# Cross attention in fp32 on one core: smaller pieces of fill, transposes as stages of their own, scores ahead of values in the last part

## The chip, the core and the metric

The kernel runs on one core of a Trainium2 chip. A core has five engines with instruction queues of their own: TensorE (PE in the profile; its weight loads are PEld), VectorE (DVE), ScalarE (ACT), GpSimd (POOL) and SyncE (SP), which here only issues DMAs. Engines wait for each other by semaphores. Each engine runs its own instructions in the order in which the program has them. The metric is the device time of one execution in microseconds (us); lower is better.

## The reference

`x` is (2, 2048, 640), the context is (2, 128, 384), of which the first 124 rows of a batch are text and the last 4 are adapter tokens; there are 8 heads of width 80. Everything is fp32.

```python
query = hidden_states @ Wq
keyt = enc @ Wk;  valt = enc @ Wv
hs = _mha(query, keyt, valt)                       # text: 2048 queries, 124 keys
ca_q1 = jnp.einsum('btc,th->bch', ca, Wq_ca)       # adapter: 384 queries
ca_q1 = ca_q1[:, indices, :]                       # spread over 2048 rows
ca_hs1 = _mha(ca_q1, residual, residual)           # 2048 keys: x itself
ca_q2 = ca_hs1 @ Wq
ca_hs2 = _mha(ca_q2, ca @ Wk_ca, ca @ Wv_ca)       # 4 keys
out = (hs + ca_hs2) @ Wout + b_out + residual
```

So there are two attentions: that of the text, with an output for each of 4096 rows, and that of the adapter, which needs only 384 different rows a batch; its result is gathered by row and added.

## The kernel before

**Two streams of work on TensorE.** The adapter is the main stream. For each batch it has *maxima* (line 782: four steps, one a block of 512 rows of x; each step is six pieces of four small matmuls `s1`, whose result of 128x2048 VectorE reduces to maxima `mx`), then *less_maxima* (line 801), then *contraction* (line 815: 2x16 pieces of four matmuls `s2`, an exponential `ea` on ScalarE, and four matmuls `acc`). Only one PSUM tile, `sq`, is there for `s1` and `s2`, so the next piece cannot start until `mx` or `ea` has read it. The time between is filled with the second stream: the text. Its pieces are *queries* (line 926, matmuls `pq`), *scores* (line 961, matmuls `sc`, on VectorE the maximum `m` and the subtraction into `p`, on ScalarE the exponential of `p`), *turned* (line 1008: VectorE transposes `p` into `eb`, which goes to HBM as `kept` and comes back as `pT`), and *values* (line 1037: matmuls `ph`, then `po` against Wout, and the sum with the residual `xo`). A unit is 256 rows of text; there are 16.

**Who sets the order.** The kernel writes TensorE's order out by hand. `pe.us` is a running estimate of the time that TensorE has been given (line 24). `weave` (line 1149) runs one piece of the adapter, takes from it a number of microseconds (`gap`), and lets `Mix.run` (line 149) take steps of the fills until as much time has been given; what was given too much is taken off the next gap. A fill is a list of stages; a stage is blocked while one of its `needs` does not hold. `Mix.until` (line 159) forces a named stage. DMAs from SyncE are kept in the order of the program too (line 245). On VectorE, ScalarE and GpSimd the framework's scheduler sets the order; `dve.behind` only forbids that one instruction goes ahead of another, and `dve.close` (line 66) puts all later ones of VectorE behind the last.

**x and its transposes.** x is needed with the channel on the partitions. `x_load` (line 714) issues eight DMAs into one staging tile, `xi` (one buffer, tag `xz`), with 32x32 blocks already in place, and `x_turn` (line 733) does the rest with five transposes on VectorE into `xt`. Because there is one staging tile, the load of a block of x waits for the five transposes of the block before. `rows_stages` (line 1189) makes a stage of each; the second waits until 24 us of TensorE's estimated time have passed since the load. `yz_block` (line 751) multiplies `xt` by the adapter's keys and values (matmuls `pyz`, a copy `yz` on ScalarE) and transposes the result into `y_sb` (matmuls `pt_y`). `setup_values` (line 602) issues ten loads of Wout into `wout_sb`, after the load of x's last block of batch 0, and then has matmuls `pvca`, `pv`, and `pw2`, which read `wout_sb`.

**The last part.** When the adapter of batch 1 has ended (line 1264), the remaining units run alone. `ahead` (line 1163) makes one stage of each unit m: `together` gives a step in turn to `turned(m+1)`, `residual(m+1)`, `completed`, the scores of unit m+2 and the values of unit m.

Of the kernel before, what the change touches and what calls it, by code (L numbers as in the profile page):

```python
# [8 lines left out]
F32 = mybir.dt.float32  # L9
# [10 lines left out]
class TensorInOrder:  # L20
# [3 lines left out]
    def __init__(self, tc):  # L24
        self.tc, self.us = tc, 0.0
# [107 lines left out]
class Mix:  # L133

    def __init__(self, pe, *fills):
        self.pe, self.fills, self.at = pe, [[f, w, f.us] for f, w in fills], None
# [20 lines left out]
    def until(self, done, what):  # L159
        while what not in done:  # L160
            for f, _, _ in self.fills:
                if any(getattr(p, "what", None) == what for p in f.parts):
                    while self.at is not None and self.at is not f and self.at.open:
                        self.at.step(self.pe)
                    self.at = f
                    if not f.step(self.pe):
                        assert what in done or self.step(), what
                    break
            else:
                assert what in done, what  # L170
# [3 lines left out]
def kernel(  # L174
# [504 lines left out]

    xt = {}  # L680
    blocks = [(b, sb) for b in range(B) for sb in range(NSB)]
    yz_of, o2_of, q_of, e_of, pT_of, xr_of, early_of = {}, {}, {}, {}, {}, {}, {}
    whole = set()
    coming = []

    def x_tile(b, sb, again):

        users = [] if again else [("yz", b, sb)]
# [43 lines left out]

    def x_turn():

        _, t, xi = coming
        coming.clear()
        most, rest = staged(xi)
        before = None
        for k in range(5):
            if k < 4:  # L740
                src = most[:, :, 4 * k : 4 * (k + 1)].rearrange("p c r a -> p c (r a)")
                ins = dve.transpose(t[:, k, :4], src)
            else:
                ins = dve.transpose(t[:, :, 4], rest.rearrange("p (k r) a -> p k (r a)", k=4))
            if before is not None:
                dve.behind(ins, before)
            before = ins
        dve.close()
        yield

    def yz_block(b, sb):
# [17 lines left out]
        for u in range(2):  # L769
            nc.scalar.activation(yz[:, u, :], ps[u], AF.Identity, bias=ones)  # L770
        yield
        for u in range(2):
            py = mm_tile(f"pt_y_{b}_{sb}_{u}")
# [182 lines left out]
    def tiles(m):  # L956

        b, m = divmod(m, NST // 2)
        return [(b, 2 * m + k) for k in range(2)]

    def scores(m):
# [3 lines left out]
        for b, st in tiles(m):  # L965
            rows = slice(st % 4 * P, (st % 4 + 1) * P)
            e = pools["e"].tile([P, HEADS, NTOK], F32, tag="e", name=f"p_{b}_{st}")
            for u in range(2):
# [18 lines left out]
                )  # L987
                if u == 0:
                    yield
            nc.scalar.activation(e[:, :, :NK], e[:, :, :NK], AF.Exp, scale=SCALE)  # L990
# [3 lines left out]
            before = b, st, e  # L994
            yield
        divided(*before)
# [11 lines left out]
    def turned(m, wait=3):  # L1008


        eb = pools["eb"].tile([P, 4, 2, HEADS, R], F32, tag="eb", name=f"eb_{m}")
        for k, at in enumerate(tiles(m)):
            last = dve.last
            ins = dve.transpose(eb[:, :, k], e_of.pop(at).rearrange("p h (j b) -> p j h b", j=4))
            dve.behind(ins, last)
        kept = hbm.tile([P, 4, 2 * HEADS * R], F32, tag="hbm", name=f"kept_{m}")
        dma(kept, eb.rearrange("p j k h a -> p j (k h a)"))
        for _ in range(wait):
# [3 lines left out]
        for j in range(4):  # L1022
            dma(pT[R * j : R * (j + 1)].rearrange("p i k h a -> p i (k h a)"), by_keys[j])
        yield

    def residual(m):
# [8 lines left out]
        yield  # L1035

    def values(m):
# [6 lines left out]
        for c0, n in ((0, 2), (2, 2), (4, 1)):  # L1044
# [16 lines left out]
            hsT += [t[:, k * N : (k + 1) * N] for k in range(n)]  # L1061
            yield
        for k, (b, st) in enumerate(tiles(m)):
# [13 lines left out]
            if ("o2", b) in done:  # L1077
                if m not in whole:
                    add_second(xr[k], b, st)
                dma(out[b, st * P : (st + 1) * P, :], xr[k])  # L1080
            else:
# [66 lines left out]

    def weave(main, fill):

        due = 0.0
        for gap in main:
            due = fill.run(due + gap)

# [5 lines left out]
    def begin(b):  # L1160
        mx_of[b] = small.tile([P, NCC, 2, 4, NSB], F32, tag="mx", name=f"mx_{b}", bufs=1)

    def ahead(m):

# [3 lines left out]
        if m + 1 < units:  # L1168
            more = [turned(m + 1), residual(m + 1)]
        more.append(completed())  # L1170
        if m + 2 < units:
            parts.append(stage(("s", m + 2), scores(m + 2)))
        n = m // 2 + 2
        if NSB <= n < len(blocks):
# [13 lines left out]

    def rows_stages(b, sb, *needs, again=False):
# [8 lines left out]
    def yz_stage(b, sb, *needs):  # L1198
        return stage(("yz", b, sb), yz_block(b, sb), *needs)
# [6 lines left out]
    own = Fill(  # L1206
        done,
        loads[0][0],
        stage("keys", setup_keys()),
        loads[0][1],  # L1210
        loads[1][0],
        yz_stage(0, 1, ("half", 0, 0)),
        loads[1][1],
        loads[2][0],
        stage("values", setup_values()),
        yz_stage(0, 2, ("half", 0, 1)),
        loads[2][1],
        yz_stage(0, 3, ("half", 0, 2)),
    )
# [3 lines left out]
    weave(setup_a2(), fill)  # L1223
    own.parts.insert(0, yz_stage(0, 0))
    for sb in range(NSB):
        fill.until(done, ("yz", 0, sb))
        weave(maxima(0, sq, mx_of[0], sb, 2.4), fill)
    fill.until(done, "values")
# [13 lines left out]
    for sb in range(2, NSB):  # L1242
        later.add(*rows_stages(1, sb, slots.free(1), ("yz", 1, 0)))
# [9 lines left out]
    own.add(  # L1253
        yz_stage(1, 0),
        *[yz_stage(1, sb, ("half", 1, sb - 1), ("x", 1, sb)) for sb in range(1, NSB)],
    )
    for sb in range(NSB):
        fill.until(done, ("yz", 1, sb))
        weave(maxima(1, sq, mx_of[1], sb, 4.8), fill)
    weave(less_maxima(1, mx_of[1]), fill)  # L1260
    ps_turns[:] = [ps_m]
    on[0] = "AD"
    weave(contraction(1, sq, 2.0), fill)
    sq_stack.close()


# [34 lines left out]
```

## Time and profile before

| What | Value |
|---|---|
| median of 3 timed runs | 758.69 us (758.14 to 760.32) |
| the profiled execution | 764.96 us |
| its span, first to last instruction | 763.3 us |
| DVE busy | 374.9 us (49%) |
| granted TensorE clock | 0.998 |
| DMA | 95.63 MB, mean 125 GB/s |

Stages by the trace: setup to about 48 us; maxima of batch 0 to 165; its contraction and output to 320; maxima of batch 1 to 478; its contraction to 620; the last units to 763. A row of the list of waits gives who waited for whom, the total in us, how often, and the longest. A row of the timeline gives start, length, engine, line, operation, out<-in, shapes, count, and in brackets the idle time of the engine before it with what ended it. L28 is the helper that records every matmul, L55 that of every VectorE operation, L247 that of every DMA of SyncE; groups are told apart by tile names (buffer numbers left out: `pw` is `pw2`, `s` is `s1` or `s2`). A row of the windows gives the stretch, its length, busy us and instructions of PE, PEld, DVE, ACT and POOL, the granted clock, the DMA share and GB/s.

### The profile page before, as it was taken

The numbers are of one execution on the slowest core, as the hardware profiler recorded it, in microseconds if no ns is written. First come the engines' busy times: TensorE is split into PE (matmuls) and PEld (weight loads), VectorE is DVE, ScalarE is ACT, GpSimd is POOL, SyncE is SP. The second block draws the span as 40 slices with busy tenths as digits, with TensorE's granted clock in tenths as the row PEclk, the third lists the DMA queues.
The fourth block names the chain that finished last, engine by engine and source line by source line (L and its number), as shares of the span: only waits on it lengthen the run. The fifth ranks groups of instructions, "written<-read, shape, count | busy, mean of one in ns | idle before, by whom it ended". The sixth has DMA issues, their size and how long they took to land.

```text
span 763.3 us, 9394 instructions
## 1 busy us (share of the span) xinstructions
PE 734.3 (96%) x3809; PEld 372.8 (49%) x3809; DVE 374.9 (49%) x506; ACT 195.3 (26%) x240; POOL 133.7 (18%) x184
## 2 busy tenths in 40 slices
PE   6989999999989999999999999999999999999997
PEld 4553343344344445555445454534433556556664
DVE  3036744653274446398749495422420616346631
ACT  2230121114343433322112110443534311011100
POOL 7000000000121012317311230010100023432320
PEclk9999999999999999999999999999999999999999
DMA  9806730000767484599995285410910527876783
GB/s 283 171 10 61 95 62 0 1 1 1 168 135 119 130 142 135 127 252 194 279 191 163 52 176 107 136 45 18 187 46 1 162 69 216 170 213 175 207 225 86
DMA packets 146853, 95.63 MB, mean 125 GB/s; under 512 B 118069, under 2 KB 118389, under 8 KB 144762
## 3 DMA queue, kind: packets, MB, share of 16 engines
q1 hardware_dynamic: 141690, 84.44, 46.8%
q0 software_dynamic: 5120, 10.59, 8.0%
q8 instruction: 30, 0.49, 0.3%
q14 instruction: 13, 0.11, 0.1%
HBM read 63.48 MB, written 31.52 MB: 124 GB/s over the span
## 4 chain that ended last, share of the span: by engine, by line
PE 87%; DVE 6%; DMA 3%; ACT 2%; issue 1%; POOL 0%; SPq 0%; DVEq 0%; ACTq 0%; POOLq 0%
PE po L28 22%; PE pq L28 22%; PE s L28 13%; PE sc L28 10%; PE acc L28 6%; PE ph L28 6%; PE pyz L28 3%; PE pk L28 1%; ACT ea L846 1%; PE pt_y L41 1%; DVE mx L55 1%; DMA pT<-kept 1%; PE pv L28 1%; DVE p L55 1%; DVE m L55 1%
## 5 line engine op out<-in xcount | busy, mean ns | idle before, releaser
L28 PE MATMUL po<-wout_sb,hsT 128*128 128x320 f32 x640 | 187.3, 438 | 0.9 <-DVE xo L55 0.6
L28 PEld LDWEIGHTS po<-wout_sb,hsT 128*128 128x128 f32 x640 | 118.3, 190 | 72.0 <-issue 28.2
L28 PE MATMUL pq<-xt,wq_sb 128*128 128x512 f32 x320 | 151.7, 610 | 0.0
L55 DVE TENSOR_REDUCE mx<-s 128x4 f32<-128x2048 f32 x48 | 109.9, 2291 | 77.7 <-PE s L28 77.7
L846 ACT ACTIVATE ea<-s 128x1536 f32<-128x1536 f32 x64 | 92.7, 1448 | 105.2 <-PE s L28 105.1
L55 DVE TENSOR_TENSOR xo<-xo,po 128x320 f32<-128x320 f32 x64 | 31.0, 484 | 152.6 <-PE po L28 152.6
L1005 POOL TENSOR_TENSOR p<-p,r 128x992 f32<-128x992 f32 x32 | 63.5, 2028 | 231.9 <-DVE r L55 223.2
L28 PE MATMUL sc<-kpad,q 128*128 128x248 f32 x384 | 95.6, 386 | 1.3 <-ACT hsT L268 0.7
L28 PEld LDWEIGHTS pq<-xt,wq_sb 128*128 128x128 f32 x320 | 58.1, 192 | 78.3 <-issue 73.0
L28 PEld LDWEIGHTS sc<-kpad,q 128*128 128x128 f32 x384 | 69.0, 190 | 32.4 <-issue 17.0
L28 PE MATMUL s<-ca,yz 32*128 32x384 f32 x512 | 59.4, 533 | 4.2 <-ACT ea L846 3.8
L268 ACT COPY q<-pq 128x512 f32<-128x512 f32 x30 | 17.6, 585 | 169.8 <-PE pq L28 169.8
L55 DVE TENSOR_REDUCE m<-sc 128x4 f32<-128x496 f32 x64 | 42.3, 663 | 33.3 <-PE sc L28 33.3
L28 PE MATMUL s<-yz,ca 32*128 32x512 f32 x384 | 54.7, 640 | 3.7 <-DVE mx L55 3.7
L1087 POOL DMA_INDIRECT xo<-o,query x25 | 39.1, 1565 | 93.3 <-DMA xo<-in_x_dram 34.9
L28 PE MATMUL acc<-ea,y_sb 128*32 128x384 f32 x512 | 55.2, 503 | 0.0
L28 PE MATMUL ph<-pT,vpad 128*32 128x256 f32 (+1 forms) x512 | 52.0, 395 | 2.4 <-DMA pT<-kept 2.1
L990 ACT ACTIVATE p<-p 128x992 f32<-128x992 f32 x32 | 33.0, 1030 | 73.9 <-DVE p L55 73.7
L55 DVE TENSOR_TENSOR p<-sc,m 128x496 f32<-128x496 f32 x64 | 42.6, 669 | 1.6
L268 ACT COPY hsT<-ph 128x512 f32<-128x512 f32 (+1 forms) x25 | 12.9, 515 | 105.6 <-PE ph L28 105.5
L55 DVE STREAM_TRANSPOSE eb<-p 128x1024 f32<-128x1024 f32 x32 | 38.0, 1222 | 2.2 <-POOL p L1005 2.2
L28 PE MATMUL pq<-xt,wq 128*128 128x512 f32 x80 | 38.0, 603 | 0.0
(142 smaller groups left out, 416.9 us busy)
## 6 DMA issues: line engine op xcount, KB each, us to landing
kept<-eb SPq DMA_DIRECT2D x16, 1024.0 KB
pT<-kept SPq DMA_DIRECT2D x64, 256.0 KB
xi<-in_x_dram SPq DMA_DIRECT2D x44, 256.0 KB
xo<-in_x_dram SPq DMA_DIRECT2D x32, 320.0 KB
out_dram<-xo SPq DMA_DIRECT2D x25, 320.0 KB
xi<-in_x_dram SPq DMA_DIRECT2D x44, 64.0 KB
early<-xo SPq DMA_DIRECT2D x7, 320.0 KB
xe<-early SPq DMA_DIRECT2D x7, 320.0 KB
```

What stands on the lines that cost most here:

```text
L28: ins = self.tc.nc.tensor.matmul(out, lhsT, rhs, **kw)
L41: ins = self.tc.nc.tensor.transpose(out, in_, ident)
L55: self.last = getattr(self.tc.nc.vector, name)(*args, **kw).ins
L268: nc.scalar.copy(dst, src)
L846: nc.scalar.activation(e, q4[:, :, :CAD], AF.Exp, scale=SCALE)
L990: nc.scalar.activation(e[:, :, :NK], e[:, :, :NK], AF.Exp, scale=SCALE)
L1005: nc.gpsimd.tensor_tensor(et, et, r.unsqueeze(2).to_broadcast([P, HEADS, NK]), ALU.mult)
L1087: nc.gpsimd.indirect_dma_start(out=t, out_offset=None, in_=o2_of[b], in_offset=bass.IndirectOffsetOnAxis(ap=query[:, st : st + 1], axis=0) ...
```

## The change

Five things are altered, all of them in the order of the work. No matmul is added or removed.

- `weave` takes a `least`: a piece of the adapter is followed by at least that much fill, whatever was given too much before (2.0 us in the maxima, 0.8 in the contraction); the gap of the first maxima is 2.3 in place of 2.4.
- The transposes of y are a stage of their own, `y_rows`, which waits until 1 us after `yz_block`. The maxima now need only `yzT`, the part before it.
- `x_turn` does one transpose a stage; the k-th waits k us longer. `Mix.until` can override these waits (`hurry`).
- In `scores` the exponential comes one piece later.
- In the last part the scores of unit m+2 go ahead of the values of unit m (two steps of scores to one of values), the three `ph` of a unit follow each other, the transposes into `eb` and the write of `kept` for the last unit move to unit 13 (`turned_out`, `out_soon`), and the last unit's outputs are written in halves.

```diff
@@ Mix.until
-                    if not f.step(self.pe):
-                        assert what in done or self.step(), what
+                    if not f.step(self.pe) and what not in done and not self.step():
+                        Mix.hurry = True
+                        assert f.step(self.pe), what
+                        Mix.hurry = False
@@ x_turn
-    def x_turn():
+    def x_turn(k):
...
+        last = dve.last
+        if k < 4:
+            src = most[:, :, 4 * k : 4 * (k + 1)].rearrange("p c r a -> p c (r a)")
+            dve.behind(dve.transpose(t[:, k, :4], src), last)
+        else:
+            src = rest.rearrange("p (k r) a -> p k (r a)", k=4)
+            dve.behind(dve.transpose(t[:, :, 4], src), last)
+            dve.close()
+            coming.clear()
         yield
@@ yz_block
-        yield
+        yz_at[b, sb] = pe.us
+        yield
+
+    def y_rows(b, sb):
+
+        yz = yz_of[b, sb]
         for u in range(2):
             py = mm_tile(f"pt_y_{b}_{sb}_{u}")
@@ scores
-                if u == 0:
-                    yield
+                yield
             nc.scalar.activation(e[:, :, :NK], e[:, :, :NK], AF.Exp, scale=SCALE)
...
             before = b, st, e
-            yield
+        yield
         divided(*before)
@@ turned
+        if m not in kept_of:
+            turned_out(m)
+        kept = kept_of.pop(m)
@@ values
-            yield
+            if c0 == 4 or not alone():
+                yield
...
-                dma(out[b, st * P : (st + 1) * P, :], xr[k])
+                for n in range(2 if m == units - 1 else 1):
+                    cols = slice(n * HALF, (n + 1) * HALF if m == units - 1 else H)
+                    dma(out[b, st * P : (st + 1) * P, cols], xr[k][:, cols])
@@ weave
-            due = fill.run(due + gap)
+            due = fill.run(max(due + gap, min(gap, least)))
@@ ahead
-            more = [turned(m + 1), residual(m + 1)]
+            more = [turned(m + 1, 1 if m + 2 == units else 3), residual(m + 1)]
...
+        if m + 3 == units:
+            parts.append(out_soon(m + 2))
...
-        return stage(("t", m), together(*more, chain(*parts), values(m)), *needs)
+        return stage(("t", m), unit(m, more, parts), *needs)
+
+    def unit(m, more, parts):
+        if alone():
+            yield from together(*more, beside(chain(*parts), values(m), 2))
+        else:
+            yield from together(*more, chain(*parts), values(m))
@@ rows_stages
-            stage(
-                ("again" if again else "x", b, sb), x_turn(),
-                lambda: not coming or pe.us > coming[0] + 24.0,
-            ),
+            *[
+                stage(
+                    (("again" if again else "x") if k == 4 else ("turned", k), b, sb), x_turn(k),
+                    lambda k=k: Mix.hurry or pe.us > coming[0] + after + k,
+                )
+                for k in range(5)
+            ],
@@ the stages of setup and the main loops
-    loads = [rows_stages(0, sb) for sb in range(1, NSB)]
+    loads = [rows_stages(0, sb, after=24.0 if sb > 1 else 18.0) for sb in range(1, NSB)]
...
-        weave(maxima(0, sq, mx_of[0], sb, 2.4), fill)
+        weave(maxima(0, sq, mx_of[0], sb, 2.3), fill, 2.0)
...
-    weave(contraction(0, sq, 2.0), fill)
+    weave(contraction(0, sq, 2.0), fill, 0.8)
...
-        weave(maxima(1, sq, mx_of[1], sb, 4.8), fill)
+        weave(maxima(1, sq, mx_of[1], sb, 4.8), fill, 2.0)
```

More of the change, by code (lines that the diff above doesn't have):

```diff
@@ L133 @@
 class Mix:
+    hurry = False
     def __init__(self, pe, *fills):
@@ L680 @@
     xt = {}
+    yz_at = {}
     blocks = [(b, sb) for b in range(B) for sb in range(NSB)]
-    yz_of, o2_of, q_of, e_of, pT_of, xr_of, early_of = {}, {}, {}, {}, {}, {}, {}
+    yz_of, o2_of, q_of, e_of, kept_of, pT_of, xr_of, early_of = [{} for _ in range(8)]
     whole = set()
@@ L686, in x_tile @@
     def x_tile(b, sb, again):
-        users = [] if again else [("yz", b, sb)]
+        users = [] if again else [("yzT", b, sb)]
         users += [("q", b, sb)] if again or b == 0 else []
@@ L731, in staged @@
         )
-    def x_turn():
+    def x_turn(k):
         _, t, xi = coming
-        coming.clear()
         most, rest = staged(xi)
[L738 to L748, printed above, removed]
+        last = dve.last
[7 more added lines that the diff above has]
+            coming.clear()
         yield
@@ L1008, in turned @@
     def turned(m, wait=3):
[L1011 to L1017, printed above, removed]
+        if m not in kept_of:
+            turned_out(m)
+        kept = kept_of.pop(m)
         for _ in range(wait):
@@ L1024, in turned, with turned_out @@
         yield
+    def turned_out(m):
+        eb = pools["eb"].tile([P, 4, 2, HEADS, R], F32, tag="eb", name=f"eb_{m}")
+        for k, at in enumerate(tiles(m)):
+            last = dve.last
+            ins = dve.transpose(eb[:, :, k], e_of.pop(at).rearrange("p h (j b) -> p j h b", j=4))
+            dve.behind(ins, last)
+        kept = kept_of[m] = hbm.tile([P, 4, 2 * HEADS * R], F32, tag="hbm", name=f"kept_{m}")
+        dma(kept, eb.rearrange("p j k h a -> p j (k h a)"))
     def residual(m):
@@ L1035, in residual, with alone @@
         yield
+    def alone():
+        return "adapter" in done
     def values(m):
@@ L1147, in chain, with weave @@
             yield from p
-    def weave(main, fill):
+    def weave(main, fill, least=0.0):
         due = 0.0
         for gap in main:
-            due = fill.run(due + gap)
+            due = fill.run(max(due + gap, min(gap, least)))
     mx_of = {}
@@ L1161, in begin, with out_soon @@
         mx_of[b] = small.tile([P, NCC, 2, 4, NSB], F32, tag="mx", name=f"mx_{b}", bufs=1)
+    def out_soon(m):
+        yield
+        turned_out(m)
+        yield
     def ahead(m):
@@ L1187, with rows_stages, yz_stages @@
     setup_z()
-    def rows_stages(b, sb, *needs, again=False):
+    def rows_stages(b, sb, *needs, again=False, after=24.0):
         return [
             stage(("load", b, sb), x_load(b, sb, again), lambda: not coming, *needs),
-            stage(
-                ("again" if again else "x", b, sb), x_turn(),
-                lambda: not coming or pe.us > coming[0] + 24.0,
-            ),
-        ]
-    def yz_stage(b, sb, *needs):
-        return stage(("yz", b, sb), yz_block(b, sb), *needs)
+            *[
[5 more added lines that the diff above has]
+            ],
+        ]
+    def yz_stages(b, sb, *needs):
+        return [
+            stage(("yzT", b, sb), yz_block(b, sb), *needs),
+            stage(("yz", b, sb), y_rows(b, sb), lambda: Mix.hurry or pe.us > yz_at[b, sb] + 1.0),
+        ]
     def early(n):
@@ L1209 @@
         stage("keys", setup_keys()),
-        loads[0][1],
+        *loads[0][1:],
         loads[1][0],
-        yz_stage(0, 1, ("half", 0, 0)),
-        loads[1][1],
+        *yz_stages(0, 1, ("half", 0, 0)),
+        *loads[1][1:],
         loads[2][0],
         stage("values", setup_values()),
-        yz_stage(0, 2, ("half", 0, 1)),
-        loads[2][1],
-        yz_stage(0, 3, ("half", 0, 2)),
+        *yz_stages(0, 2, ("half", 0, 1)),
+        *loads[2][1:],
+        *yz_stages(0, 3, ("half", 0, 2)),
     )
@@ L1223 @@
     weave(setup_a2(), fill)
-    own.parts.insert(0, yz_stage(0, 0))
+    own.parts[:0] = yz_stages(0, 0)
     for sb in range(NSB):
-        fill.until(done, ("yz", 0, sb))
-        weave(maxima(0, sq, mx_of[0], sb, 2.4), fill)
+        fill.until(done, ("yzT", 0, sb))
+        weave(maxima(0, sq, mx_of[0], sb, 2.3), fill, 2.0)
+    fill.until(done, ("yz", 0, NSB - 1))
     fill.until(done, "values")
@@ L1242 @@
     for sb in range(2, NSB):
-        later.add(*rows_stages(1, sb, slots.free(1), ("yz", 1, 0)))
+        later.add(*rows_stages(1, sb, slots.free(1), ("yzT", 1, 0)))
     for sb in range(1, NSB):
@@ L1253 @@
     own.add(
-        yz_stage(1, 0),
-        *[yz_stage(1, sb, ("half", 1, sb - 1), ("x", 1, sb)) for sb in range(1, NSB)],
+        *yz_stages(1, 0),
+        *[p for sb in range(1, NSB) for p in yz_stages(1, sb, ("half", 1, sb - 1), ("x", 1, sb))],
     )
     for sb in range(NSB):
-        fill.until(done, ("yz", 1, sb))
-        weave(maxima(1, sq, mx_of[1], sb, 4.8), fill)
+        fill.until(done, ("yzT", 1, sb))
+        weave(maxima(1, sq, mx_of[1], sb, 4.8), fill, 2.0)
     weave(less_maxima(1, mx_of[1]), fill)
+    fill.until(done, ("yz", 1, NSB - 1))
     ps_turns[:] = [ps_m]
     on[0] = "AD"
-    weave(contraction(1, sq, 2.0), fill)
+    weave(contraction(1, sq, 2.0), fill, 0.8)
     sq_stack.close()
+    done.add("adapter")
     ps_rest = ctx.enter_context(tc.tile_pool(name="ps_r", bufs=4, space=bass.MemoryType.PSUM))
```

## The prediction

> **What bounds the kernel now.** The page came first (busy shares), then the list of waits of TensorE (PE), then the timeline around each wait, then the DMA windows.
>
> ```profile
> span 763.3 us, 9394 instructions
> PE 734.3 (96%) x3809; PEld 372.8 (49%) x3809; DVE 374.9 (49%) x506; ACT 195.3 (26%) x240; POOL 133.7 (18%) x184
> PE s L28 <- ACT ea L846: 3.8, 5, 1.8
> PE s L28 <- DVE mx L55: 3.7, 4, 1.4
> PE pt_y L41 <- ACT yz L770: 3.1, 4, 0.8
> PE ph L28 <- DMA pT<-kept: 2.1, 1, 2.1
> ```
>
> PE is busy 96% of the span and its instructions run in one written order, so the kernel lasts as long as PE streams plus what it waits. The page counts 29.0 us without a matmul; the four kinds of waits above are 12.7 us of it, and they are what the change could remove. Any wait that the new order adds to PE's one queue moves the end by its whole length.
>
> The second reading is the loads of setup, because VectorE, SyncE's queue and PE form one chain there:
>
> ```profile
> 79.30 3.07 DVE L55 STREAM_TRANSPOSE xt<-xi 128x512 f32<-128x512 f32 x5
> ...
> 97.35 2.29 DVE L55 TENSOR_REDUCE mx<-s 128x4 f32<-128x2048 f32 x1 [1.55 <-PE s L28]
> ...
> 103.49 3.08 DVE L55 STREAM_TRANSPOSE xt<-xi 128x512 f32<-128x512 f32 x5
> ...
> 82.40 2.04 SPq L247 DMA_DIRECT2D xi<-in_x_dram  x2
> ...
> SPq L247 <- DVE xt L55: 15.1, 1, 15.1
> ...
> 91.11 10.14 SPq L247 DMA_DIRECT2D wout_sb<-in_L_xattn_Wout_dram  x10
> ...
> 107.71 0.27 PE L41 MATMUL pt_vca<-ident,vca 128*128 128x128 f32 x1
> ...
> 109.00 2.89 PE L28 MATMUL pw<-wout_sb,blk_v 128*32 128x320 f32 x20 [0.84 <-DVE blk_v L55]
> ```
>
> There is one staging buffer (xi, tag xz). SyncE waited 15.1 us for the transposes of x's block 2 to leave it, issued block 3 at 82.40, 0.03 us after they ended, and only behind those eight issues, at 91.11, the ten loads of Wout. The DMA windows say how long this takes:
>
> ```profile
> 82.40:91.10 8.70, 7.45 (x29) 2.67 (x28) 5.89 (x3) 0.58 (x1) 0.00 (x0) 1.00 0.99 123
> 91.10:102.00 10.90, 10.90 (x64) 4.22 (x64) 6.16 (x4) 1.52 (x4) 0.00 (x0) 1.00 1.05 171
> 102.00:103.00 1.00, 1.00 (x5) 0.70 (x4) 1.00 (x1) 0.00 (x0) 0.00 (x0) 1.00 0.09 21
> 103.00:109.00 6.00, 5.16 (x29) 3.43 (x27) 4.17 (x10) 2.20 (x12) 0.00 (x0) 1.00 0.00 1
> ```
>
> The last two columns are the DMA share and GB/s: the engines are full from 82.4 to 102 and empty by 103. So Wout is complete 20.3 us after the transposes of block 2 end (82.37 to some 102.7; 102 and 103 are the bounds). The product pw2 that reads it starts at 109.0, with 6.3 us to spare.
>
> **The change part by part.** Places come from the order of the built program.
>
> *Transposes of x one at a time (the term that decides).* On VectorE the five transposes of block 2 stood ahead of mx(0,1,0,0), the first maximum of step 1. They now stand behind mx(0,1,2,0), five maxima later, still next to each other. SyncE's order is the same: block 3, then Wout. PE's order is the same too in what matters: s1(0,1,2,0), s1(0,1,2,1), the twelve pv, then pw2. So I follow the chain. Three waits on mx ahead of this place go (the PE gaps of 0.50 at 68.05, 0.53 at 79.44 and 1.25 at 84.61: 2.28 us). The maximum of 97.35 then ends at 97.35 + 2.29 - 2.28 = 97.4, the transposes (3.07) at 100.4, Wout at 100.4 + 20.3 = 120.7. PE comes to pw2 earlier: 2.28 less 0.56, because between s1(0,1,2,0) and s1(0,1,2,1) only one pq and pvca are left (1.07 + 0.96 + 0.95 = 2.98 us, against the 3.55 us between the s at 64.49 and 68.05, which mx sets). The matmul of pw2 that needs all of Wout started at 109.68 (109.00 + 0.68 for the four before it); it could start at 107.96 and must stay until 120.7. That is 12.8 us of stall, against 1.7 us won. Bounds for the stall: 12.1 to 13.1, from the landing alone. Nothing hides it: the pq, pyz and s behind pw2 are ready, but PE takes them in order.
>
> *The same in block 3.* Its transposes stood behind mx(0,1,2,1), under the pv at 103.49, at no cost. Now they stand behind mx(0,2,1,1), and pyz of block 3 comes two pq after s1(0,2,1,1). From that s: 1.21 to its maximum, 2.29, then four transposes (4 x 0.61) = 5.95, against 1.07 + 1.81 of PE work: 3.1 us of wait. The wait of 1.39 at 136.89 goes, since two pq are put there. Net +1.7 (the fifth transpose adds 0.6 at most; if the old wait stays, 1.4).
>
> *Transposes of y a stage of their own.* PE waited four times 0.77 us between pyz and pt_y for the copy of yz. In three of the four places s1 now follows pyz at once, and it reads yz as well, so the wait stays and only its owner changes. One goes: -0.8 (bounds -3.1 and 0).
>
> *Least fill, and exponentials a piece later.* The middle of the kernel (165 to 622 us) has 7.5 us of waits of PE: 3.8 on ea, the rest on ca, p, xo, hsT, o and r. Least fill puts at least 0.8 us of text between two steps of the contraction; the 1.03 us exponential of text moves behind the next scores. In the new order I still find a text exponential just ahead of an ea with little PE work in three places (0.5, 0.5 and 1.3, as the 0.4 to 1.8 of now). New are: the second ph of unit 0, whose buffer is freed by a subtraction of VectorE that stands behind two eb transposes (2 x 1.25 and the 0.56 between them at 220.38, less 1.35 of sc: 1.7); ph of unit 3, the same place with less work before it (2.6); and the second pm, behind a maximum and a subtraction (0.67 + 0.55, some 1.1). Sum 7.7 against 7.5: +0.2, bounds -4 (all ea waits gone) and +3 (each new one twice).
>
> *Scores first in the last part, hsT in one go.* Matmuls on 128x128 alternate with tiled ones (rows or columns of 32 or 64). From s at 88.45 to s at 92.29 are 3.84 us; inside are four concurrent s (0.86) and three pq (3 x 0.86), 3.44 together. So one way there and back costs 0.40, 0.20 a change. I count 385 changes before, 368 after: -3.4 (bounds -1.7, if a change costs 0.1 as the first pq after an s does, and -5). The Trainium skill, "TensorEngine Tiling (Array Packing)", section Key Properties, says that changing the tiling mode drains the engine. It names no price, so by it alone the sum would only lose this term's size, not its sign; the 0.40 us agrees with it.
>
> *The last unit.* PE waits 2.1 us at 745.3 for pT, whose chain (eb at 729.76, kept, pT) begins with unit 14's end. Now eb and kept are issued in unit 13 and pT waits one step instead of three: -2.1 (0 if the reload of two xo ahead of it in SyncE's queue is late). The last two outputs go in halves, four issues for two of 0.33 us each. From the last issue's end at 760.1 to the span's end are 3.2 us that no engine's work covers; a half may take less of it, one more issue may add 0.33: I take 0, between -1.6 (half of it) and +0.3. The Trainium skill, "DMA: Bandwidth & Descriptors", section Anatomy of one DMA, gives some 2.0 us fixed and the bytes at 436 GB/s; by an estimate from it a half of 160 KB lands 0.4 us before a whole, and the sum would be 0.4 lower. No row here shows a half.
>
> Sum: +12.8 - 1.7 + 1.7 - 0.8 + 0.2 - 3.4 - 2.1 = **+6.7 us**. The profiled execution took 764.96 (span 763.3), 6.3 above the median 758.69 of the three timed runs; the change is added to the median: 758.7 + 6.7 = **765.4 us**.
>
> **The rivals.** Within 0.3% of 758.7 (756.4 to 761.0) a measurement of this kernel can't tell a change from none.
>
> *Wout is not late* (faster). If the transposes of block 2 ran where they did, or the loads of Wout did not queue behind block 3, the 12.8 would be gone and the rest is -6.1: 752.6. It decides once Wout lands before 108. Against it: the order of the built program and the 0.03 us between the transposes' end and the next issue. Chance 0.06.
>
> *Late x, and more behind it* (slower still). The chain of block 3 is as late as Wout, and the new waits on VectorE's queue come at the upper bounds: 13.1 + 2.3 + 3, changes at -1.7, pT's wait stays, and only 1.7 and 0.8 are won: +14.2, 772.9. For it: the waits on eb transposes. Against: after the stall every load has 12 us more. Chance 0.17.
>
> *Stall, but the gains come whole.* Stall 12.1, ea waits gone (-4), changes -5, the rest as summed: 12.1 - 1.7 + 1.7 - 3.1 - 4 - 5 - 2.1 = -2.1, that is 756.6, "the same". Half of these gains gives 761. Chance 0.12, mostly near the half.
>
> *Nothing changes*: the new order cancels by itself; no row speaks for it. Counted with the last.
>
> **How the numbers follow.** The forecast has 0.65. It spreads by the bounds of its terms, some 4 us either way (middle -4/+3, changes 1.7): 761.4 to 769.5. The range takes in half of the rival above and the nearer half of the one below: 760.4 to 771.4. Faster: 0.06 and a little of the third, 0.08. Same: the rest of the third, 0.08. Slower 0.84.
>
> **What would show it.** In the profile after: xt of block 2 at about 97 to 101; SyncE's first Wout issue at about 109; a PE wait at pw of some 12 us on the DMA of wout_sb, the longest of the run; a wait of about 3 us of pyz on xt near 145; pT's wait gone; PE busy some 3 us less. Wrong would be: pw without that wait (then faster), or new waits on DMA anywhere in the loads of the second batch.

## The result

The changed kernel takes 769.21 us (median of 5 runs), the kernel before, timed beside it, 760.2 us (median of 5). The ratio is 1.0128, with a 95% interval of 1.0088 to 1.0169: it is slower, by about 9.0 us or 1.3%, where +6.7 was forecast. (A sixth run of the changed kernel, of 773.69 us, is on record outside these five.) Of the 3.8 us between 765.4 and 769.2, 1.5 are the base (758.7 in the three runs shown, 760.2 in five) and 2.3 the change.

### The profile page after: what moved, and what is told of

It reads as the page before. It is cut to its first block, busy times and chain, and to the rows that moved or that the text cites. A ratio compares the mean times of both kernels' runs of the same rounds, so it can differ in the third digit from the quotient of the medians.

```text
span 763.8 us, 9412 instructions
## 1 busy us (share of the span) xinstructions
PE 726.9 (95%) x3809; PEld 372.4 (49%) x3809; DVE 376.7 (49%) x507; ACT 193.4 (25%) x239; POOL 133.3 (17%) x184
## 4 chain that ended last, share of the span: by engine, by line
PE 91%; DVE 2%; issue 2%; DMA 2%; SPq 2%; ACT 1%; POOL 0%; DVEq 0%; ACTq 0%; POOLq 0%
PE po L28 24%; PE pq L28 23%; PE s L28 13%; PE sc L28 11%; PE acc L28 6%; PE ph L28 6%; PE pyz L28 3%; SPq L251 2%; DMA wout_sb<-in_L_xattn_Wout_dram 1%; PE pt_y L41 1%; PE pk L28 1%; DVE xt L55 1%; DMA xz<-in_x_dram 1%; PE pw L28 1%; ACT ea L853 1%
## 5 line engine op out<-in xcount | busy, mean ns | idle before, releaser
L28 PE MATMUL pq<-xt,wq_sb 128*128 128x512 f32 x320 | 150.0, 603 | 0.0
L853 ACT ACTIVATE ea<-s 128x1536 f32<-128x1536 f32 x64 | 92.6, 1447 | 99.0 <-PE s L28 99.0
L1011 POOL TENSOR_TENSOR p<-p,r 128x992 f32<-128x992 f32 x32 | 61.6, 1991 | 246.5 <-DVE r L55 246.4
L28 PE MATMUL sc<-kpad,q 128*128 128x248 f32 x384 | 93.6, 384 | 0.0
L28 PE MATMUL ph<-pT,vpad 128*32 128x256 f32 (+1 forms) x512 | 50.0, 387 | 4.2 <-issue 2.4
L1106 POOL DMA_INDIRECT xo<-o,query x23 | 35.9, 1562 | 87.2 <-DMA xo<-in_x_dram 47.4
L55 DVE TENSOR_REDUCE r<-p 128x8 f32<-128x992 f32 (+1 forms) x34 | 37.5, 1108 | 0.3 <-ACT p L887 0.3
```

What stands on the lines that cost most here:

```text
L28: ins = self.tc.nc.tensor.matmul(out, lhsT, rhs, **kw)
L55: self.last = getattr(self.tc.nc.vector, name)(*args, **kw).ins
L853: nc.scalar.activation(e, q4[:, :, :CAD], AF.Exp, scale=SCALE)
L1011: nc.gpsimd.tensor_tensor(et, et, r.unsqueeze(2).to_broadcast([P, HEADS, NK]), ALU.mult)
L1106: nc.gpsimd.indirect_dma_start(out=t, out_offset=None, in_=o2_of[b], in_offset=bass.IndirectOffsetOnAxis(ap=query[:, st : st + 1], axis=0) ...
```

## The profile after

The profiled execution took 765.52 us. The page's span and busy line, and then the list of TensorE's waits (line numbers have moved by a few; L853 is the exponential `ea`, L772 the copy `yz`):

```profile
span 763.8 us, 9412 instructions
PE 726.9 (95%) x3809; PEld 372.4 (49%) x3809; DVE 376.7 (49%) x507; ACT 193.4 (25%) x239; POOL 133.3 (17%) x184
...
PEclk9999968999999999999999999999999999999999
```

```profile
PE pw L28 <- DMA wout_sb<-in_L_xattn_Wout_dram: 13.8, 1, 13.8
...
PE pyz L28 <- DVE xt L55: 3.0, 1, 3.0
PE ph L28 <- issue: 2.4, 1, 2.4
PE s L28 <- ACT ea L853: 2.3, 3, 1.3
PE ph L28 <- DVE p L55: 1.8, 1, 1.8
PE s L28 <- ACT yz L772: 1.5, 2, 0.8
```

One wait is by far the longest, and it is new: `pw2` waits 13.85 us for Wout. The waits of `pt_y` on `yz` and of the last unit on `pT` are gone, those on `mx` fell from 3.7 to 0.4 us. The timeline shows the chain that the prediction followed, and its windows how the engines stood meanwhile (the columns are those of the windows before):

```profile
92.20 3.07 DVE L55 STREAM_TRANSPOSE xt<-xi 128x512 f32<-128x512 f32 x5
...
95.30 9.34 SPq L251 DMA_DIRECT2D xi<-in_x_dram  x8
...
104.69 9.78 SPq L251 DMA_DIRECT2D wout_sb<-in_L_xattn_Wout_dram  x10
114.28 1.30 PE L28 MATMUL pw<-wout_sb,blk_v 128*32 128x320 f32 x8 [13.85 <-DMA wout_sb<-in_L_xattn_Wout_dram]
...
116.31 3.85 PE L28 MATMUL pw<-wout_sb,blk_v 128*128 128x320 f32 x12 [0.73 <-issue]
```

```profile
95.27:104.60 9.33, 5.16 (x28) 3.39 (x26) 2.79 (x6) 2.20 (x12) 0.00 (x0) 0.90 1.07 120
104.60:114.30 9.70, 0.02 (x4) 0.05 (x5) 0.00 (x0) 0.00 (x0) 0.00 (x0) 0.50 1.12 185
114.30:116.30 2.00, 1.27 (x8) 0.20 (x9) 0.00 (x0) 0.00 (x0) 0.00 (x0) 0.50 0.08 23
116.30:120.00 3.70, 3.69 (x12) 1.18 (x12) 0.00 (x0) 0.42 (x1) 0.00 (x0) 0.52 0.02 4
120.00:124.00 4.00, 3.23 (x17) 0.94 (x20) 0.00 (x0) 1.32 (x3) 0.86 (x3) 1.00 0.00 0
```

The transposes of block 2 end at 95.27, block 3 is issued at 95.30, Wout at 104.69, and TensorE, idle since 100.43, starts the first matmul that needs all of it at 116.31, 21.0 us after the transposes. The column before the last two is the granted clock: it is 0.50 until 120. So `pw2` itself, which took 2.89 us before, takes 1.30 + 3.85 us. No step of the prediction had that.

**Two things blur a comparison of spans.** The spans differ by only 0.5 us (763.8 against 763.3), the medians by 9.0. First, the end of setup varies from execution to execution: in the profile before, the first `pt_a2` starts at 49.66, after, at 44.27; among the thirteen profiled executions of this study it lies anywhere between 44.1 and 50.0. Most of that is the clock as well. Its record at full speed begins at 16.5 us in the profile before and at 7.2 in the one after; a matmul of setup (`pt_x` from `x_last`) takes 0.42 us ahead of that time and 0.27 behind it. Of TensorE's work ahead of `pt_a2`, 10.1 us fell outside full speed in the one and 2.9 in the other, which is 3.6 of the 5.4 us between them; 1.7 more is longer waiting. Without that loss the thirteen lie within 2.6 us instead of 5.8. Second, the half clock comes and goes later on too. So I use for each kernel the time from the start of the first `pt_a2` to the end of the last matmul (M), and M less half of the time that TensorE was busy at half clock in it (M'). Both are worked out from the trace of one profiled execution:

| Kernel | M | PE idle in M | busy at half clock | M' | median of runs |
|---|---|---|---|---|---|
| before | 709.6 | 17.4 | 3.4 | 707.9 | 760.2 |
| after | 716.3 | 28.0 | 4.9 | 713.8 | 769.2 |
| e1, Wout issued earlier | 703.5 | 14.2 | 6.6 | 700.2 | 753.2 |
| e2, x^T in one stage | 699.8 | 13.5 | 0 | 699.8 | 751.4 |
| e3, busy wait, 30 matmuls | 722.5 | 14.0 | 12.9 | 716.1 | 772.2 |
| e4, x^T's part alone, on before | 728.9 | 32.9 | 12.1 | 722.9 | 781.2 |
| e5, e2 with the last part as before | 704.8 | 14.8 | 3.4 | 703.1 | 756.9 |
| e6, e2 with text and fill as before | 706.5 | 18.2 | 2.6 | 705.2 | 757.4 |
| e7, busy wait, 24 matmuls | 716.9 | 16.0 | 3.4 | 715.2 | 772.5 |
| e8, e2 with eb a unit earlier | 705.6 | 16.2 | 3.4 | 703.9 | 756.3 |
| e9, e2 without least fill | 708.4 | 20.9 | 0 | 708.4 | 763.2 |
| e10, e2 with exponentials as before | 697.4 | 11.2 | 0 | 697.4 | 749.3 |
| e11, e2 with y in one stage | 703.3 | 15.6 | 0 | 703.3 | 755.4 |

From before to after M' grows by 5.9 us: idle time grows by 10.6, busy time less the half clock falls from 690.5 to 685.8.

## The experiments

**e1: is it Wout's place behind block 3?** The ten loads (and the one of the bias) are taken out of `setup_values` into a stage of their own ahead of the load of block 3; the order of TensorE and VectorE is unchanged.

```diff
+        stage("wout", setup_wout()),
         loads[2][0],
         stage("values", setup_values()),
```

> The changed kernel with one edit: the ten loads of Wout are issued ahead of the loads of x's block 3, so they no longer wait for the staging buffer. The order on TensorE, VectorE and of everything else on SyncE's queue stays. Theory (Wout queued behind block 3 is the cause): the wait of pw on Wout (13.85 us, with the 0.73 behind it) is gone, pw's twenty matmuls take 2.9 us again instead of 5.2, and the time falls by 14 to 17 us against the changed kernel, to some 753, below the kernel before by about 7. The wait of pyz of block 3 on xt stays at about 3.0. Rival 1 (the stall only hides other lateness, such as x's loads of the second batch, which have 12 us less then): the gain is under 8 us, 761 or more, and new waits on DMA stand further on. Rival 2 (pw is held by something else than Wout, such as blk_v): the wait keeps most of its length, 768.

Measured: 753.2 us, ratio to before 0.9899 (0.9862 to 0.9936). The timeline of e1:

```profile
59.36 9.80 SPq L251 DMA_DIRECT2D wout_sb<-in_L_xattn_Wout_dram  x10
...
96.29 10.80 SPq L251 DMA_DIRECT2D xi<-in_x_dram  x8
...
102.26 2.89 PE L28 MATMUL pw<-wout_sb,blk_v 128*32 128x320 f32 x20 [0.84 <-DVE blk_v L55]
...
126.39 4.54 PE L28 MATMUL pyz<-xt,wyz 128*64 128x512 f32 x12 [2.99 <-DVE xt L55]
```

Wout is issued at 59, the wait is gone, `pw2` takes 2.89 again, and M' falls by 13.6 (713.8 to 700.2): 14.6 of wait gone, 0.84 on `blk_v` come back. All other waits are those of the changed kernel. Nothing behind the stall was hidden by it. The wait of 3.0 on `xt` stays, as expected; this time the clock falls behind it, and `pyz` takes 4.54 us instead of 3.00.

**e2: the other parts without this one.** The five transposes of x^T are one stage again.

```diff
-            *[
-                stage(
-                    (("again" if again else "x") if k == 4 else ("turned", k), b, sb), x_turn(k),
-                    lambda k=k: Mix.hurry or pe.us > coming[0] + after + k,
-                )
-                for k in range(5)
-            ],
+            stage(
+                ("again" if again else "x", b, sb), x_turn(),
+                lambda: Mix.hurry or not coming or pe.us > coming[0] + 24.0,
+            ),
```

> The changed kernel with one part undone: the five transposes of x^T are again one stage, as before the change; the rest of the change stays. Theory: the transposes of block 2 stand ahead of mx(0,1,0,0) again, so Wout lands some 20 us behind them and ahead of pw. The 13.85 + 0.73 of wait, some 2.3 of slow pw and the 2.99 of pyz on xt go; the waits on mx come back (1.9 more than now) and the old wait of pyz (1.4): 769.2 - 19.9 + 3.3 = 752.6, with 750 to 756 as bounds. That is also the sum of the prediction without its first term. Rival (the rest of the change is worth nothing by itself, and only the whole moves the time): the time of the kernel before, 758 to 760. Rival 2 (the rest of the change costs something): above 761.

Measured: 751.35 us, ratio 0.9885 (0.9843 to 0.9927). M' is 14.1 below that of the changed kernel and 8.1 below that of the kernel before. The waits of e2:

```profile
PE ph L28 <- issue: 1.8, 1, 1.8
PE ph L28 <- DVE p L55: 1.8, 1, 1.8
PE s L28 <- ACT ea L856: 1.8, 2, 1.3
PE s L28 <- ACT yz L775: 1.5, 2, 0.8
PE s L28 <- DVE mx L55: 1.4, 2, 1.0
PE po L28 <- DVE xo L55: 1.3, 1, 1.3
```

The waits on Wout and on `xt` are not there, those on `mx` are back by 1.0. So the change is a gain of 8.1 us with a loss of 14.1 laid over it, and the loss is this one part.

**e4: this part alone, on the kernel before.**

```diff
-            stage(
-                ("again" if again else "x", b, sb), x_turn(),
...
+            *[
+                stage(
+                    (("again" if again else "x") if k == 4 else ("turned", k), b, sb), x_turn(k),
+                    lambda k=k: Mix.hurry or pe.us > coming[0] + after + k,
```

> The kernel before with one part of the change alone: the transposes of x^T are five stages, with the changed conditions; nothing else. On VectorE those of block 2 stand behind mx(0,1,2,0) and those of block 3 behind mx(0,2,1,1), as in the changed kernel. Theory (this part carries the loss): the wait of pw on Wout is 12 to 15 us, pw takes some 2.3 us more by the half clock, pyz of block 3 waits some 3 us: +12.8 by the prediction's terms for this part (12.8 - 1.7 + 1.7), +15 with the slow pw, so 772 to 776, more than the whole change costs. Rival (the loss comes from the parts together, as the least fill moves pw forward): under +6, 766 or less. Rival 2 (it is the y and text parts): no change.

Measured: 781.23 us, ratio 1.0291 (1.0247 to 1.0335), 20.7 us slower: above the 772 to 776 expected. The timeline of e4's TensorE:

```profile
115.27 1.29 PE L28 MATMUL pw<-wout_sb,blk_v 128*32 128x320 f32 x8 [12.97 <-DMA wout_sb<-in_L_xattn_Wout_dram]
...
117.42 4.00 PE L28 MATMUL pw<-wout_sb,blk_v 128*128 128x320 f32 x12 [0.85 <-issue]
...
144.50 5.67 PE L28 MATMUL pyz<-xt,wyz 128*64 128x512 f32 x12 [3.85 <-DVE xt L55]
```

Both waits are there without any other part of the change, so none of the others is needed for them. M' grows by 15.0, as the waits say, where the expectation had 12.8. The clock comes on top: after both waits it stands at half, for 17.07 and 6.83 us, of which TensorE was busy 12.1, a loss of 6.0 against 1.7 in the profile before, so 4.3 more, where the expectation had 2.3. The two make up 4.2 of the 5.7 us by which it fell short; the rest stays open.

**e3 and e7: is the low clock TensorE's idleness?** Thirty, then 24 matmuls of ready operands ahead of `pw2` keep TensorE busy while it waits. They write the tile that `pw2` starts anew. The diff is that of e3. (In the trace one such matmul stands as two records, so thirty are x60.)

```diff
             pw = mm_tile(f"pw2_{u}")[:, :HALF]
+            for _ in range(30 if u == 0 else 0):
+                tc.keep_in_program_order(
+                    nc.tensor.matmul(pw, ident, w_c["v"][:, 0, :HALF], start=True, stop=True)
+                )
```

> The changed kernel with thirty matmuls of 128x320 (437 ns each by the row of po, 13.1 us together) ahead of the first of pw. They write the same PSUM tile, which pw then starts anew. TensorE is busy while it waits for Wout. Theory (the clock that the throttle grants fell because TensorE stood idle for 14 us): the stretch of 17 us at half clock is gone, pw's twenty matmuls take 2.9 us instead of 5.2, and the time is 1.5 to 3 us lower than that of the changed kernel, with the end of pw at the same place otherwise. Rival (the low clock has another cause, such as the load of the DMA engines or power): pw stays at 5.2 us, and the time does not fall. If the matmuls end after Wout lands, up to 1 us is added to either.

> The busy wait again, with 24 matmuls in place of 30. In the run with 30 one took 547 ns, so they ended 2.4 us past the time at which Wout had landed (some 114.7); 24 take 13.1 us, from 100.8 to 113.9, just short of it. All else is the changed kernel. Theory (the low clock comes from TensorE's idleness): no stretch at half clock between 100 and 120; pw's twenty matmuls take 2.9 us; they end 2.0 to 2.8 us earlier than in the changed kernel, counted from the arrival at pw, and the time is 1.5 to 3 below its 769.2. Rival (only a wait turned into work, the clock is not the cause): pw at 5 us, same time.

The windows of e3 and its timeline:

```profile
104.00:108.00 4.00, 4.00 (x17) 2.81 (x16) 0.00 (x0) 0.00 (x0) 0.00 (x0) 1.00 0.79 117
108.00:112.00 4.00, 4.00 (x17) 2.81 (x16) 0.00 (x0) 0.00 (x0) 0.00 (x0) 1.00 1.00 229
```

```profile
100.80 16.42 PE L675 MATMUL pw<-w_v,ident 128*128 128x320 f32 x60
117.15 2.89 PE L28 MATMUL pw<-wout_sb,blk_v 128*32 128x320 f32 x20
```

The DMA share (0.79 and 1.00) is near that of the stall (1.07 and 1.12), and the clock is 1.00: it is the idleness, not the load of the DMA engines. `pw2` takes 2.89 us. In e7 too no half clock lies in this stretch. But no time was won (772.2 and 772.5): in e3 the thirty took 16.4 us and ended past the landing; in e7 the last pieces of Wout still came 1.24 and 1.34 us late, and from the arrival at `pw2` to the first `pyz` were 18.6 us, 1.0 less than the 19.6 of the changed kernel, where 2.0 to 2.8 were expected. Elsewhere, behind shorter waits (below), e3 lost 6.4 us to the half clock and e7 1.7. So the cause of the low clock is shown; that a busy wait pays is not.

**e5: the last part as before**, on top of e2.

```diff
     def alone():
-        return "adapter" in done
+        return False
...
-            more = [turned(m + 1, 1 if m + 2 == units else 3), residual(m + 1)]
+            more = [turned(m + 1), residual(m + 1)]
...
-        if m + 3 == units:
-            parts.append(out_soon(m + 2))
...
-                for n in range(2 if m == units - 1 else 1):
-                    cols = slice(n * HALF, (n + 1) * HALF if m == units - 1 else H)
-                    dma(out[b, st * P : (st + 1) * P, cols], xr[k][:, cols])
+                dma(out[b, st * P : (st + 1) * P, :], xr[k])
```

> The changed kernel with the transposes of x^T in one stage, and in addition the last part as before the change: no scores first, hsT with a step between its pieces, pT of the last unit not ahead, the last outputs whole. To be held against the run with the transposes in one stage alone (751.35 us; there the stretch from the first ph of unit 10 to that of unit 15 is 108.5 us, against 113.9 before the change). Theory of the prediction: the wait of 2.1 on pT comes back, and twelve changes of tiling mode more (380 against 368, all in the last part) at 0.20 each are 2.4: +4.5, 755.9. Rival 1 (the changes cost nothing, and the rest of the gain was a better overlap on VectorE): +2.1, 753.4. Rival 2 (more per change than 0.20, as the two traces' 5.4 for this stretch suggest: (5.4 - 2.1)/12 = 0.27): +5.4, 756.8. The halves of the last outputs: the stretch from the last product's end to the end of the span changes by between -0.3 and +1.6.

Measured: 756.89 us, ratio 0.9949 (0.9921 to 0.9977). In M' the last part is worth 3.3: 1.3 of idle time, which is `pT`'s wait

```profile
PE ph L28 <- DMA pT<-kept: 1.3, 1, 1.3
```

and 2.0 of busy time, 0.17 for each of the twelve changes of tiling mode if they make all of it, which is not shown (below). The 3.3 lie between the theory's 4.5 and rival 1's 2.1. The medians differ by 5.5, as rival 2 had it, but the profiled run of e5 lost 1.7 us to the half clock and that of e2 none. The end of the last matmul lies 3.8 us ahead of the span's end, against 3.3 in e2 with the outputs in halves.

**e6, e9, e10: the least fill and the later exponentials**, on top of e2: both undone, the first alone, the second alone. The diff shows one of the four calls of `weave` that lose their least fill (e6 and e9), and the step in `scores` (e6 and e10).

```diff
-    weave(contraction(0, sq, 2.0), fill, 0.8)
+    weave(contraction(0, sq, 2.0), fill)
...
-                yield
+                if u == 0:
+                    yield
```

> The changed kernel with the transposes of x^T in one stage, and in addition without the least fill and with the exponentials of text where they were. To be held against 751.35 us, the run with the transposes in one stage alone. Theory of the prediction: these parts are worth +0.2 in waits and take away six changes of tiling mode (374 against 368), 1.2 us: the time rises by 1.0, 752.4, with waits on ea of 3 to 4 us in place of 1.8 and the two waits of ph of 1.8 gone or moved. Rival (the least fill is what keeps the waits on ea small): +3 or more, 754.5. Rival 2 (the later exponentials only cost): the time falls by 1 to 3.

> The changed kernel with the transposes of x^T in one stage, and without the least fill; the exponentials of text stay where the change puts them. Undoing both cost 5.4 us (from pt_a2 to the last product 705.2 in place of 699.8, without what the half clock took), where the prediction had +0.2 for the two and 1.2 for six changes of tiling mode. Theory now (the least fill is the part that counts: it puts TensorE's work between an s and the maximum or exponential that frees its buffer): 4 to 6 us more than 699.8 in this measure, with waits of s on mx of 4 to 6 us in place of 1.4 and on ea of more than 2.8. By the prediction: 7 changes x 0.20 = 1.4, and within 1 us in waits. Rival (the two parts only help together): under 2.

> The changed kernel with the transposes of x^T in one stage, and with the exponentials of text where they were before the change; the least fill stays. The number of changes of tiling mode is the same, 368. Theory now (the least fill is the part that counts): within 1.5 us of 699.8 in the measure from pt_a2 to the last product without the half clock. Prediction: the later exponentials move the waits on ea and add the two waits of ph behind eb (1.7 and 2.6), so undoing them takes those away and brings back about as much on ea: within 2. Rival (the exponentials are the part that counts): +3 to +6, with waits on ea of 4 to 7 us.

Measured: e6 757.36 us (ratio 0.9932, 0.9906 to 0.9958), e9 763.16 us (1.0024, 0.9988 to 1.0059), e10 749.31 us (0.9838, 0.9788 to 0.9889). In M' against e2: +5.4, +8.6 and -2.4. The waits of e9, then of e10:

```profile
PE s L28 <- DVE mx L55: 5.8, 8, 1.8
...
PE sc L28 <- DVE p L55: 3.2, 1, 3.2
PE acc L28 <- ACT ea L856: 3.0, 1, 3.0
```

```profile
PE s L28 <- ACT ea L856: 1.5, 2, 1.0
PE s L28 <- DVE mx L55: 1.4, 2, 1.0
```

Without the least fill the waits on `mx` are 5.8 in place of 1.4, and a `sc` and an `acc` wait 3 us each. So the least fill is the most valuable part, and it works by putting TensorE's work where it would wait; its 8.6 is more than the 4 to 6 expected. In e6 the waits on `mx` are 5.8 too. The later exponentials cost 2.4 us in M' (the times alone do not show it: 748.98 to 749.9 in e10, 748.75 to 757.67 in e2): the waits on `xo` (1.3) and of `acc` on `ea` (1.0), which e2 has, are not in e10. Both waits of `ph` stay in e10, so it is not the later exponentials that make them, as its expectation had it.

**e11: y in one stage**, on top of e2.

```diff
     def yz_stages(b, sb, *needs):
-        return [stage(("yzT", b, sb), yz_block(b, sb), *needs),
-                stage(("yz", b, sb), y_rows(b, sb), ...)]
+        return [stage(("yz", b, sb), chain(yz_block(b, sb), y_rows(b, sb)), *needs)]
```

> The changed kernel with the transposes of x^T in one stage, and with the transposes of y in one stage with yz, as before the change. 371 changes of tiling mode in place of 368. Prediction: three waits of pt_y on yz of 0.77 in place of two of s on yz, and one or two more: +0.8 (0 to 3.1), and 0.6 for the three changes, together +1.4: 701.2 in the measure from pt_a2 to the last product without the half clock. Rival (the stage of its own only moves work): within 0.5 of 699.8. Rival 2 (s of the next step is later, so that its maximum is late): +3.

Measured: 755.42 us, ratio 0.9921 (0.9894 to 0.9949). M' is 3.5 above e2, near rival 2's size, but not by its mechanism: the waits on `mx` fell to 0.4.

```profile
PE pt_y L41 <- ACT yz L775: 3.9, 5, 0.8
...
PE sc L28 <- DVE p L55: 1.1, 1, 1.1
```

Five waits of `pt_y` on `yz` (3.9) stand in place of those of `s` (1.5, and 0.8 that the list of e2 counts as issue), `sc` waits 1.1, `pT` is waited for 0.5, `mx` 1.0 less: +2.2 (idle time grew by 2.1). Busy time grew by 1.4.

**e8: a try at something faster.** The units from 1 on issue `eb` at the end of their own scores, as the change does for the last one.

```diff
-        if m + 3 == units:
+        if m + 2 < units:
             parts.append(out_soon(m + 2))
...
-        together(turned(0, 1), stage(("s", 1), scores(1)), residual(0)),
+        together(turned(0, 1), chain(stage(("s", 1), scores(1)), out_soon(1)), residual(0)),
```

> The changed kernel with the transposes of x^T in one stage, and with the transposes eb of every unit issued at the end of the scores of that unit, a unit earlier, as the change does for the last unit alone. It is meant to be faster than all others. Theory (the two waits of ph come from subtractions that stand behind eb on VectorE's queue): the wait of ph in unit 3 (1.8 us in the run to be held against) is gone, that of unit 0, whose eb stays where it was, stays; 751.35 - 1.8 = 749.5. Rival (eb now waits for GpSimd's division in the middle of a unit, and the additions to xo and the copies of hsT behind it are late): new waits of po or ph on VectorE in units 1 to 12, and a time of 752 or more.

Measured: 756.3 us, ratio 0.9945 (0.992 to 0.997). The wait of `ph` in unit 3 falls from 1.8 to 0.5, but the rival won: M' is 4.1 above e2, with new waits on VectorE's queue and for `pT`, among them

```profile
PE po L28 <- DVE xo L55: 2.1, 2, 1.8
...
PE ph L28 <- DMA pT<-kept: 0.8, 1, 0.8
PE po L28 <- DVE hsT L55: 0.8, 1, 0.8
```

**The fastest version** is e10: least fill, y in stages of its own and the changed last part, with x^T's transposes in one stage and the exponentials where they were: 749.31 us, 1.6% below the kernel before, 2.6% below the changed one (749.31 / 769.21). Its lead over e2 rests on M', as said above.

## Why the prediction was right, and where it was not

**Wout behind block 3 (+12.8, less 1.7).** Right in every link: transposes, block 3's issues, Wout's issues, wait. The wait was 13.85 + 0.73 = 14.6, above the upper bound of 13.1. Three sizes were off. The last load of Wout was issued at 114.16 and landed 1.7 us later, at 115.9, that is 20.6 us after the transposes, not 20.3; the matmul that needs it started another 0.4 later, for which the prediction had nothing. The wait of 0.84 for `blk_v`, which stood ahead of `pw2` before, now lies inside the stall. And TensorE came to `pw2` 5.2 us after the transposes' end (100.43 against 95.27), where the prediction had 6.9 (107.96 less 0.68, against 100.4): it was earlier than thought, and the part of the wait that comes of this costs nothing by itself. The places were right too: with the 5.4 us by which setup ended earlier in this execution added, the transposes are at 97.6 (97 was said) and the first issue of Wout at 110.1 (109).

**Block 3's transposes (+3.1, -1.39).** The wait of `pyz` is 2.99. This and the term above, 12.8 together, measure 14.1 on the changed kernel (e2) and 15.0 on the one before (e4).

**The waits of the middle (+0.2).** Each new wait is there at its place and nearly its size: `ph` of unit 0 1.8 (1.7), `ph` of unit 3 2.4 (2.6), the second `pm` 0.9 (1.1), three on `ea` 2.3 in all (2.3).

**The rest of the gains (-0.8, -3.4, -2.1; with the middle -6.1).** Measured -8.1 in M' (e2). Idle time fell by 3.9 where the prediction had 2.7, busy time without the half clock by 4.2 (690.5 to 686.3) where it had 3.4 for 17 changes of tiling mode. That would be 0.25 a change, against 0.20 predicted and 0.17 in e5. But that the changes of mode make this busy time is not shown: e8 has the same 368 changes as e2 and 1.4 us more of it, e11 three more changes and also 1.4. So the sign of the term is right, and its price stays an estimate. (On the page PE is busy 7.4 us less, where some 3 were said; 3.5 of it lie in setup.) The term of `y` came at its size: three waits of `s` (2.3 in all) stand where four of `pt_y` (3.1) were. The last unit's wait is gone, as predicted; undone alone in e5, it comes back with 1.3. The halves of the last outputs were put at 0. The last output lands 2.33 us after the last matmul's end in the profile after and 2.70 in the one before (2.32 to 2.34 in all ten profiles with halves, 2.70 or 2.71 in the three without): they gave 0.4. The estimate of 0.4 by "DMA: Bandwidth & Descriptors" agrees, though the page gives its fit for DMAs issued from GpSimd, and these are issued from SyncE. The span ends 3.3 us after the last matmul, in the profile before 4.0; what lies behind the landing differs too.

These parts are not a sum. Undone one by one from e2 they cost 3.5 (y), 5.4 (fill and exponentials) and 3.3 (last part), 12.2 together, but all of them only 8.1. The prediction read its terms from the whole new order and not from each edit, so this did not hurt it. Had it been asked for the least fill alone, its +0.2 of waits would have been wrong by 7: in e9 TensorE's idle time is 7.4 above e2's.

**Luck in the total.** The loss was 1.3 to 2.2 larger than its 12.8 and the gains 2.0 larger than their 6.1, so the two errors nearly cancel in M' (+5.9 against +6.7). What the 9.0 of the medians has above 5.9 must lie outside M', in the clock and in setup, which the sum did not have.

**The clock: the term that was missing.** The stall cost more than its length, since TensorE runs at half clock until the period ends. In the profiled execution 4.9 us of work fell in it, 2.4 us lost, against 1.7 in the profile before. The other timed executions of the changed kernel show a mean clock of 0.984 in place of 0.989, that is 24.6 us at half clock (2 x 0.016 x 767.5) and not 17.1, two periods more of at most 1.7 us loss each. With +5.9 in M', this accounts for a change above 6.7; how much of the 9.0 is setup and how much clock the times alone cannot tell. The Trainium skill's "TensorE: Matmul & The Clock Gate" has the rule that the prediction needed (Part 1, What's actually happening): half rate after an idle window of about 3.4 us, and back after a busy one. The length of that window, 3,413 ns on the page, is the step that the traces show (below). A forecast of a stall of 12 us should have added the work that falls in the periods until the clock is back: 4.9 us of it here and 6.6 in e4, 2.4 and 3.3 us lost.

**The rivals.** "Wout is not late" was priced at 752.6; made true in e1 and e2 it gave 753.2 and 751.4. Against the kernel before in the same runs (760.5) that is -7.3 and -9.2 where the price was -6.1, so the price was good to some 3 us and its condition did not hold. "Late x, and more behind it" did not come: after the stall no load of the second batch was waited for. The whole gains of the third did not come either: 2.3 us on `ea` stayed.

## What to carry to other kernels

Moving VectorE work behind other VectorE work moves every DMA that waits for the buffer it frees, and all that is queued behind that DMA: follow the queue to its last issue, here ten loads that had nothing to do with the moved transposes. Issuing what needs no buffer ahead of what does (e1) cures it as well as moving the work back (e2). A change that bundles several parts should be priced, and then undone, part by part: here a loss of 14 us outweighed a gain of 8, and inside the gain one part cost 2.4.

## What the hardware showed that was not expected

**The granted clock falls for whole periods of 3.413 us.** Every stretch at half clock between the end of setup and the last matmul, in all thirteen profiles, lasted 3.413, 6.827 or 17.067 us: one, two or five periods. Behind the stall on Wout it was five in both kernels that had it whole (the changed one, and e4), and none in e3 and e7, where TensorE was kept busy. In the changed kernel it began 2.4 us into the stall and ended 3.6 us after the first matmul that needs all of Wout had started (102.8 to 119.9).

**What decides, as far as these traces show, is how busy a whole period was, not how long a wait was.** The records of the clock give the ends of the periods, and so a grid of 3.413 us through each trace. TensorE's busy time was summed in every period between setup and the last matmul. Over all thirteen profiles, the clock fell after each of the nine periods (at full clock) with under 1.47 us busy, after 4 of the 16 with 1.47 to 1.77, and after none with more. So the same wait can cost nothing or a period at half clock, by where it lies on the grid. The wait of 2.99 on `xt` lay across an end of a period in the changed kernel (1.47 and 2.37 us busy in the two) and had no effect; in e1 it lay within one (0.69 busy), and the clock fell. The one of 2.43 at unit 3's `ph` had none in the changed kernel (2.50 and 1.89), and did in e1 (1.12). In the profile before, even a wait of 1.79 at 225.4, for an exponential, was followed by a period at half clock (1.62 busy in its own), as the windows show:

```profile
225.00:228.10 3.10, 1.30 (x14) 0.39 (x16) 1.60 (x3) 2.12 (x2) 0.00 (x0) 1.00 0.73 254
228.10:231.50 3.40, 3.40 (x25) 1.35 (x26) 0.27 (x1) 1.45 (x1) 0.00 (x0) 0.51 0.00 0
```

TensorE is busy all through the second window, at half clock, and loses 1.7 us. The clock-gate page (Why this matters for your kernels) asks for no gaps over some 3 us; here gaps from 1.8 us on were followed by a whole period at half clock at times. So a wait of 2 us has a second price of up to 1.7 us, paid in some executions and not in others. Part of the scatter between runs of one kernel may be this: the runs of the kernel before have mean clocks from 0.994 to 1.000. Why periods of 1.62 us went both ways stays open.
